# Attention with image prompts on one core: last keys in two column halves, context 1 turned by VectorE, prompt weights and x loaded from the POOL queue, and the last quarter of the first inner products sent ahead

## The chip, the cores and the metric

The kernel runs on one core of a Trainium2 chip. The core has a matrix engine (TensorE, PE in the rows, with PEld for its weight loads), a vector engine (VectorE, DVE), an activation engine (ScalarE, ACT), a general engine (GpSimd, POOL) and a synchronising engine (SyncE, SP) that mostly issues transfers. 16 DMA engines move data between main memory and the core's memories. Each engine works through its own instruction stream in order. The metric is the device time of one execution in microseconds. Three runs of the kernel before took 419.8, 420.98 and 421.6 us; the median is 420.98 us.

## The reference

Eight batches of 112 query rows (320 channels) attend, with 20 heads of 16 channels, to 371 text rows and 4 image-prompt rows of 512 channels. All is float32.

```python
q    = heads(x @ W_q);  k_t = heads(text @ W_k);  v_t = heads(text @ W_v)
p    = softmax(q k_t^T / 4)                       # (b, h, 112, 371)
text_out = p v_t
k_ip, v_ip = heads(ip @ W_k_ip), heads(ip @ W_v_ip)
qsem = l2norm(p text)                             # a 512-vector per (b, h, s)
sem  = qsem . l2norm(ip)                          # (b, h, 112, 4)
p_ip = softmax(q k_ip^T / 4 + 0.5 sem) * spatial_mask
out  = (text_out + p_ip v_ip) @ W_out + b_out + x
```

The kernel never forms qsem. With G = text text^T (the inner products, or Gram matrix), |p text|^2 = p G p^T, and (p text) . ip_n = p (text ip_n), so one product of the probabilities with the columns [G | text ip_n | 1 | V] gives everything that is needed of them.

## The kernel before, in words

**Steps.** A step is (batch b, group g): four heads at a time, five groups to a batch, 40 steps. `scores` (L652) multiplies the masked queries `qm` with the transposed keys `kT`; four heads lie in four 32-row strips of the array, 16 rows of each strip being real and the other 16 masked to zero (two heads share a strip, and r picks one). `probabilities` (L671) takes the maximum on DVE, the exponential on ACT, and SP sends the result p in rows of 32 to the buffer `xg` (`xg<-p`, L686). `transposed` (L688) turns it on DVE in 32x32 blocks into `xgT`. `product` (L703) multiplies `xgT`, block by block, with `u`, which holds [G | text ip_n | 1 | V] for the group. `reduced` (L759) sums product times p on DVE, `value_sums` (L734) copies the rest on ACT. `finish` (L780) makes the output of a batch.

**What feeds u.** `gram` (L463; `first_gram`, L433, for batch 0) computes the inner products, `doubled` scales them into `ug` on ACT and POOL, and `gram_to_groups` (L484) sends each quarter of `ug` with four SP transfers into `u`. `values` (L535) computes V into `vext`; it goes to main memory (`vd`) and comes back by groups (`vr`, `values_to_groups`, L578); `placed` (L625) copies it on POOL into `u`.

**Context.** `ctxT`, the transposed context, is made from `ct`. For batches 0 and 1 `load_ctx` (L135) loads whole rows and `transposed_context` (L394) turns them on PE and copies them out; for batches 2 to 7 the context is loaded in blocks of 32 rows by 128 channels (512-byte pieces, four transfers for the full blocks and four for the last 19 rows) and turned on DVE. `prompts_behind` (L388) lets POOL copy the normalised prompts into the last four columns.

**Keys of the last group.** Channels 256 to 319 hold only four heads. In batches 0 and 7 they come from a product with a widened key weight. In batches 1 to 6 `values` carries 64 extra columns (the key weight's last channels stand beside the value weight in `wv_sb`), POOL spreads them into `k3`, and `keys` (L493) turns them with three PE transposes.

**Order.** PE, SP, DVE, ACT and POOL are written in order by hand, first the prologue (L1020 to L1064), then the steps: `alone` (L1107) for step 0, `pair` (L1115) for two steps at a time, and after every second step `behind` (L1183), which places the coming batch's work: keys `k`, queries `q`, values `v`, inner products `gr`, transposes `tr`, endings `f`. `turn` lists which PSUM pool each next bank is taken from. The prologue's order around the change is

```python
order_values(); drain(products)
gram_to_groups(0, range(QN - 1))          # three quarters
... values(0), queries(0), values_to_dram(0), spread(...), keys(0) ...
values_to_groups(0)
... scores and probabilities of step (0, 0) ...
gram_to_groups(0, (QN - 1,))              # the last quarter
drain(transposed_context(1)); prompts_behind(1)
... scores and probabilities of step (0, 1) ...
load_embed(nc.sync, wkip_sb, w_k_ip); load_embed(nc.sync, wvip_sb, w_v_ip)
transposed(0, 0); placed(0, 0); keys(0); more_constants(); gram(1), first third
```

`project_queries` (L319) begins by letting POOL clear the unused rows of `xT` (L327), which every query product reads.

## Time and profile before

| what | value |
|---|---|
| median of three runs | 420.98 us |
| the profiled execution | 421.54 us |
| its span | 419.8 us |
| PE busy | 411.7 us (98%) |
| PE weight loads busy | 314.1 us (75%) |
| DVE busy | 322.2 us (77%) |
| ACT busy | 185.5 us (44%) |
| POOL busy | 116.0 us (28%) |
| moved by DMA | 64.64 MB in 58002 packets |

A row of the chain or of the timeline gives the start in us, the length in us, the engine, the line and the tile that is written; xN is the number of instructions merged into it, and what stands in brackets is how long the engine stood idle before it and what ended that. A float32 matrix product appears as two PE instructions. PE's ends are modelled from the instruction, so the start of the next piece says more than the end of the last. An SPq or POOLq entry is a queue issuing a transfer.

### The profile page before, as it was taken

To read this page: it belongs to the slowest core of one execution; us is meant where nothing else is said; L and a number is where in the kernel's file an instruction comes from. 1 tells how busy PE (TensorE), PEld (TensorE's weight loads), DVE (VectorE), ACT (ScalarE), POOL (GpSimd) and SP (SyncE) were. 2 spreads that over 40 slices of the span, in tenths; PEclk is the share of its full clock that TensorE was granted. 3 is DMA by queue.
4 is the path that set the end of the run, shared out by engine and by line. 5 is a ranking of instruction groups with operands and counts; after the bars stand their busy time and mean duration, and the time that the engine had idled before them with its cause. 6 is when DMAs were issued, how large, how long until landed. Compare 5 with 4: busy or idle time off the path is not lost.

```text
span 419.8 us, 13826 instructions
## 1 busy us (share of the span) xinstructions
PE 411.7 (98%) x5511; PEld 314.1 (75%) x5511; DVE 322.2 (77%) x684; ACT 185.5 (44%) x634; POOL 116.0 (28%) x278
## 2 busy tenths in 40 slices
PE   8999999999999999999999999999999999999995
PEld 8866686877677786868686877778776888776893
DVE  4054777897887876886888897887788897789964
ACT  3253333334543642514553464333643464246772
POOL 4302310031161352012051225102124126005570
PEclk9999999999999999999999999999999999999999
DMA  8678966778554656577645575575656345575311
GB/s 249 163 190 246 220 157 165 180 187 181 133 156 125 169 127 170 143 162 160 174 116 138 148 173 144 156 186 138 164 150 168 92 118 149 156 177 169 98 34 29
DMA packets 58002, 64.64 MB, mean 154 GB/s; under 512 B 19016, under 2 KB 51760, under 8 KB 57938
## 3 DMA queue, kind: packets, MB, share of 16 engines
q1 hardware_dynamic: 57054, 62.32, 58.5%
q8 instruction: 44, 0.72, 0.7%
q10 hardware_dynamic: 692, 0.89, 0.7%
q0 software_dynamic: 192, 0.55, 0.6%
q14 instruction: 20, 0.16, 0.1%
HBM read 19.04 MB, written 5.22 MB: 58 GB/s over the span
## 4 chain that ended last, share of the span: by engine, by line
PE 87%; DVE 4%; DMA 3%; ACT 2%; SPq 2%; issue 1%; ACTq 0%; POOL 0%; DVEq 0%; POOLq 0%
PE ps_qd L710 39%; PE ps_v L543 15%; PE ps_k L512 10%; PE ps_g L474 8%; PE ps_s L662 5%; PE ps_q L344 3%; PE ps_o L867 2%; DMA xg<-p 1%; DVE xgT L698 1%; PE ps_g L444 1%; DMA vr<-vd 1%; ACT p L679 1%; PE ps_c L414 1%; DVE nmx L675 1%; SPq L488 1%; DMA ct<-in_ctx_dram 1%
## 5 line engine op out<-in xcount | busy, mean ns | idle before, releaser
L710 PE MATMUL ps_qd<-u,xgT 32*112 32x40 f32 (+11 forms) x3840 | 215.7, 351 | 0.4 <-DVE xgT L698 0.4
L710 PEld LDWEIGHTS ps_qd<-u,xgT 32*112 32x112 f32 x3840 | 177.4, 172 | 38.4 <-issue 7.1
L698 DVE STREAM_TRANSPOSE xgT<-xg 128x768 f32<-128x768 f32 (+1 forms) x63 | 123.1, 1976 | 7.1 <-DMA xg<-p 7.1
L679 ACT ACTIVATE p<-ps_s,nmx 112x371 f32<-112x371 f32 x160 | 85.6, 584 | 58.3 <-DVE nmx L675 57.2
L675 DVE TENSOR_REDUCE nmx<-ps_s 112x1 f32<-112x371 f32 x160 | 77.1, 534 | 36.7 <-PE ps_s L662 34.0
L763 DVE CUSTOM_DVE_ANT_0 p<-ps_qd,p 112x371 f32<-112x371 f32 x150 | 72.7, 544 | 15.9 <-ACT pvs L737 10.4
L629 POOL COPY u<-vr 128x64 f32<-128x64 f32 x120 | 26.7, 236 | 185.0 <-PE ps_qd L710 108.0
L543 PE MATMUL ps_v<-wv_sb,ctxT 128*128 128x384 f32 (+1 forms) x192 | 63.8, 479 | 0.3 <-ACT kT L519 0.3
L662 PE MATMUL ps_s<-kT,qm 32*112 32x375 f32 (+1 forms) x320 | 60.8, 486 | 0.0
L543 PEld LDWEIGHTS ps_v<-wv_sb,ctxT 128*128 128x128 f32 x192 | 35.3, 190 | 21.2 <-ACT kT L519 1.2
L512 PE MATMUL ps_k<-ctxT,wk_sb 128*128 128x371 f32 x136 | 45.8, 481 | 0.0
L737 ACT COPY pvs<-ps_qd 112x21 f32<-112x21 f32 x150 | 21.7, 198 | 52.4 <-DVE ss L763 50.1
L512 PEld LDWEIGHTS ps_k<-ctxT,wk_sb 128*128 128x128 f32 x136 | 24.6, 190 | 13.4 <-ACT ctxT L424 0.5
L474 PE MATMUL ps_g<-ctxT 128*32 128x119 f32 (+11 forms) x672 | 33.3, 344 | 0.6 <-POOL ctxT L390 0.6
L474 PEld LDWEIGHTS ps_g<-ctxT 128*32 128x32 f32 x672 | 25.9, 109 | 8.1 <-issue 4.1
L662 PEld LDWEIGHTS ps_s<-kT,qm 32*112 32x112 f32 x320 | 27.1, 171 | 5.0 <-issue 0.5
L550 ACT COPY vext<-ps_v 128x384 f32<-128x384 f32 (+1 forms) x24 | 11.2, 465 | 37.1 <-PE ps_v L543 37.0
L681 ACT COPY ipl<-ps_s 112x4 f32<-112x4 f32 x140 | 24.0, 172 | 0.0
L353 DVE TENSOR_SCALAR qm<-ps_q,emask 128x224 f32<-128x224 f32 (+1 forms) x25 | 9.0, 398 | 18.5 <-PE ps_q L344 18.5
L460 ACT ACTIVATE ug<-ps_g 128x375 f32<-128x375 f32 (+2 forms) x24 | 9.0, 377 | 29.2 <-DMA ct<-in_ctx_dram 8.4
L519 ACT COPY kT<-ps_k 128x371 f32<-128x371 f32 x17 | 8.0, 469 | 30.5 <-PE ps_k L512 30.5
L402 DVE STREAM_TRANSPOSE ctxT<-ct 128x512 f32<-128x512 f32 x18 | 19.3, 1077 | 0.0
(157 smaller groups left out, 311.6 us busy)
## 6 DMA issues: line engine op xcount, KB each, us to landing
xg<-p SPq DMA_DIRECT2D x158, 162.3 KB
u<-ug SPq DMA_DIRECT2D x128, 99.0 KB
ct<-in_ctx_dram SPq DMA_DIRECT2D x24, 176.0 KB
vip<-vipd SPq DMA_DIRECT2D x7, 560.0 KB
vr<-vd SPq DMA_DIRECT2D x20, 120.0 KB
vd<-vext SPq DMA_DIRECT2D x14, 160.0 KB
vd<-vext SPq DMA_DIRECT2D x28, 40.0 KB
ct<-in_ctx_dram SPq DMA_DIRECT2D x4, 256.0 KB
```

Of the source, the lines that this page charges most:

```text
L474: nc.tensor.matmul(ps[p * RG : (p + 1) * RG, s0 : T - t0], ctxT[:, e, t0 + q * RG : t0 + (q + 1) * RG], ctxT[:, e, t0 + s0 : T], start=(e ...
L512: nc.tensor.matmul(ps[:, :TT], wk_sb[:, e, i * P : (i + 1) * P], s["ctxT"][:, e, :TT], start=(e == 0), stop=(e == NE - 1),)
L543: nc.tensor.matmul(ps[:, :w], ctxT[:, e, c * P : (c + 1) * P], wv_sb[:, e, :w], start=(e == 0), stop=(e == NE - 1),)
L629: nc.gpsimd.tensor_copy(region(b, c)[:, :, UV - c * P :], s["vr"][:, c * QN : (c + 1) * QN, g, :])
L662: nc.tensor.matmul(ps[:S, :w], qm[a * RG : (a + 1) * RG, i, r, j * S : (j + 1) * S], s["kT"][a * RG : (a + 1) * RG, i, :w], start=True, st ...
L675: nc.vector.tensor_reduce(nmx, ps[:S, :TT], AX.X, ALU.max, negate=True)
L679: nc.scalar.activation(p, ps[:S, :TT], AF.Exp, bias=nmx)
L681: nc.scalar.copy(s["ipl"][:, groups[g][a], :], ps[:S, TT:T])
L698: nc.vector.transpose(xT[:, j : j + n].rearrange("p j (k q) -> p q j k", q=QN), xg[:, :, j * RG : (j + n) * RG].rearrange("p q (j k) -> p ...
L710: nc.tensor.matmul(banks[a][:S, j * RG : UW], xT[a * RG : (a + 1) * RG, j, :S], region(b, c)[a * RG : (a + 1) * RG, p, q * RG :], start=(j ...
L737: nc.scalar.copy(s["pvs"][:, h, :], ps[:S, TT:UW])
L763: nc.vector.tensor_tensor_reduce(out=p, in0=ps[:S, :TT], in1=p, scale=1.0, scalar=0.0, op0=ALU.mult, op1=ALU.add, accum_out=s["ss"][:, h : ...
```

## The change

Six things change together.

1. The last group's keys. The 64 extra value columns, `k3`, `spread` and the transposes go. For every batch `last_keys` multiplies the 64 key-weight columns with the context's first 186 columns into PSUM partitions 0 to 63 and with the other 185 into 64 to 127, and four ACT copies put both halves twice into `kT`, so that partitions 64 to 127 repeat the four heads. The scores of that group take r = a // 2, and a third masked query product is made.
2. Context 1 is loaded in 32-row blocks and turned on DVE, like batches 2 to 7, and that comes right behind the first inner products, before the transfers to `u`.
3. All four quarters of the first inner products go to `u` at once, ahead of values and probabilities of step (0, 0).
4. The prompt weights and x[1:5] are loaded from the POOL queue, before the last third of the first inner products; x[5:] from the POOL queue in batch 2.
5. All of `gram(1)` is done in the prologue. The prompt projection writes four column tiles of 160 columns in place of two of 320, with three ACT copies and two transfers.
6. ACT is asked for the Sqrt table right behind the key copies, ahead of the Sqrt.

```diff
-    groups.append([2 * HC + a for a in range(GROUP)])
+    groups.append([2 * HC + 2 * (a % 2) + a // 2 for a in range(GROUP)])
...
-    def spread(eng, t):
-
-        v = t[:, :, FULL * P :].rearrange("p k (a r d) -> p k a r d", r=2, d=D)
-        for a in (3, 2, 1):
-            eng.tensor_copy(v[:, :, a, 0, :], v[:, :, a // 2, a % 2, :])
-        eng.memset(v[:, :, :, 1, :], 0.0)
...
-        if b >= LEAD:
+        if b > 0:
...
         ps = bank("ps_kv")
         for e in range(NE):
             for i, w in enumerate((wkip_sb, wvip_sb)):
-                nc.tensor.matmul(
-                    ps[i * N : (i + 1) * N, :C],
-                    ipT[:, e, :],
-                    w[:, e, :],
-                    start=(e == 0),
-                    stop=(e == NE - 1),
-                )
...
+                for n, part in enumerate(parts):
+                    m = 2 * i + n
+                    nc.tensor.matmul(
+                        ps[m * N : (m + 1) * N, : C // 2],
+                        ipT[:, e, :],
+                        w[:, e, part],
+                        start=(e == 0),
+                        stop=(e == NE - 1),
+                    )
...
-        nc.sync.dma_start(vipd, kv[N:])
+        for n, part in enumerate(parts):
+            m = 2 + n
+            nc.sync.dma_start(vipd[:, part], kv[m * N : (m + 1) * N, : C // 2])
...
-            for r in range(2 if i < FULL else 1):
+            for r in range(2):
...
-        if b >= LEAD:
+        if b > 0:
...
             if c == NT - 1:
                 nc.gpsimd.tensor_copy(ctxT[:, :, TT:T], ipnT[:, :, :NIP])
+                load_embed(nc.gpsimd, wkip_sb, w_k_ip)
+                load_embed(nc.gpsimd, wvip_sb, w_v_ip)
+                nc.gpsimd.dma_start(x_sb[:, 1:5, :], x[1:5].rearrange("b s c -> s b c"))
             c0, c1 = c * P, min(c * P + P, T)
...
-        for i in range(NC):
-            ps = bank(f"ps_k_{b}_{i}", spare=0 < b < B - 1 and i == FULL)
-            if 0 < b < B - 1 and i == FULL:
-
-                for c in range(NT):
-                    rows = min(P, TT - c * P)
-                    nc.tensor.transpose(
-                        ps[:, c * P : c * P + rows],
-                        s["k3"][:rows, c].rearrange("p a r d -> p (a r d)"),
-                        ident[:rows, :rows],
-                    )
-                nc.scalar.copy(s["kT"][:, i, :TT], ps[:, :TT])
-                yield
-                return
+        for i in range(FULL):
+            ps = bank(f"ps_k_{b}_{i}")
...
+        last_keys(b, bank(f"ps_k_{b}_{FULL}", spare=0 < b < B - 1))
+        yield
 
     def last_keys(b, ps):
 
         s = st[b]
         for e in range(NE):
-            nc.tensor.matmul(
-                ps[:, :TT],
-                wk_sb[:, e, FULL * P :],
-                s["ctxT"][:, e, :TT],
-                start=(e == 0),
-                stop=(e == NE - 1),
-            )
-        nc.scalar.copy(s["kT"][:, FULL, :TT], ps[:, :TT])
+            for n in range(2):
+                nc.tensor.matmul(
+                    ps[n * REST : (n + 1) * REST, : min((n + 1) * KH, TT) - n * KH],
+                    wk_sb[:, e, FULL * P :],
+                    s["ctxT"][:, e, n * KH : min((n + 1) * KH, TT)],
+                    start=(e == 0),
+                    stop=(e == NE - 1),
+                )
+        for n in range(2):
+            t = slice(n * KH, min((n + 1) * KH, TT))
+            for m in range(2):
+                nc.scalar.copy(
+                    s["kT"][m * REST : (m + 1) * REST, FULL, t],
+                    ps[n * REST : (n + 1) * REST, : t.stop - t.start],
+                )
 
...
-        w = C + REST if 0 < b < B - 1 else C
...
                 nc.tensor.matmul(
-                    ps[:, :w],
+                    ps[:, :C],
                     ctxT[:, e, c * P : (c + 1) * P],
-                    wv_sb[:, e, :w],
+                    wv_sb[:, e, :],
...
-            nc.scalar.copy(vext[:, c, :w], ps[:, :w])
-            if w > C and c == NT - 1:
-                nc.gpsimd.tensor_copy(
-                    s["k3"][:, :, :, 0, :],
-                    vext[:, :, C:].rearrange("p c (a d) -> p c a d", d=D),
-                )
+            nc.scalar.copy(vext[:, c, :], ps[:, :C])
...
+        if i == FULL:
+            r = a // 2
         nc.tensor.matmul(
             ps[:S, :w],
             qm[a * RG : (a + 1) * RG, i, r, j * S : (j + 1) * S],
...
     order_values()
     drain(products)
-    gram_to_groups(0, range(QN - 1))
+    drain(transposed_context(1))
+    gram_to_groups(0, range(QN))
     run(("v", 0), lambda: values(0))
     run(("q", 0), lambda: project_queries(pairs[0]), 3)
     run(("v", 0), None, 2)
     values_to_dram(0, nc.scalar)
-    spread(nc.gpsimd, wq_sb)
-    nc.gpsimd.tensor_copy(wv_sb[:, :, C:], wk_sb[:, :, FULL * P : C])
-    spread(nc.gpsimd, wk_sb)
+    nc.gpsimd.tensor_copy(wq_sb[:, :, C:], wq_sb[:, :, FULL * P : C])
...
-    gram_to_groups(0, (QN - 1,))
     run(("q", 0), None)
-    turn[:] = ["mm", "qd", "qd"]
-    drain(transposed_context(1))
-    prompts_behind(1)
     for a in range(GROUP):
         scores(0, 1, a, early=True)
         probabilities(0, 1, a)
-    load_embed(nc.sync, wkip_sb, w_k_ip)
-    load_embed(nc.sync, wvip_sb, w_v_ip)
     transposed(0, 0)
     placed(0, 0)
     run(("k", 0), None, 2)
     more_constants()
-    run(("g", 1), lambda: gram(1))
+    turn[:] = ["mm", "mm", "sc"]
+    run(("g", 1), lambda: gram(1), NT)
     prologue.close()
...
         if b % 2 == 0 and g == 0:
             if n == 0:
-                turn[:] = ["sc", "mm", "qd", "mm"]
-                nc.sync.dma_start(x_sb[:, 1:5, :], x[1:5].rearrange("b s c -> s b c"))
+                turn[:] = ["qd", "mm"]
             else:
                 turn[:] = ["qd"] * 4 + ["mm"]
                 k(b)
+                nc.scalar.preload_act_table(AF.Sqrt)
                 f(b - 1)
                 if b - 1 < B - 2:
                     prompt_values(b - 1)
             if n:
                 gr(nb)
             tr(0)
-            gr(nb, 2)
             if n:
+                gr(nb, 2)
                 f(b - 1)
             else:
                 run(("pp",), prompt_projections)
@@ -1232,8 +1211,8 @@
                 run(("pp",), None)
             tr(1)
             values_to_dram(nb, nc.sync)
-            if b == 0:
-                nc.sync.dma_start(x_sb[:, 5:, :], x[5:].rearrange("b s c -> s b c"))
+            if b == 2:
+                nc.gpsimd.dma_start(x_sb[:, 5:, :], x[5:].rearrange("b s c -> s b c"))
...
             k(b)
+            nc.scalar.preload_act_table(AF.Sqrt)
             k(nb)
```

More of the change, by code (lines that the diff above doesn't have):

```diff
@@ L52 @@
     HN = H * NIP
+    KH = (TT + 1) // 2
     VW = NIP + 1 + D
@@ L104 @@
     wq_sb = const.tile([P, NC, CP], F32, tag="wq_sb", name="wq_sb")
-    wk_sb = const.tile([P, NE, CP], F32, tag="wk_sb", name="wk_sb")
-    wv_sb = const.tile([P, NE, C + REST], F32, tag="wv_sb", name="wv_sb")
+    wk_sb = const.tile([P, NE, C], F32, tag="wk_sb", name="wk_sb")
+    wv_sb = const.tile([P, NE, C], F32, tag="wv_sb", name="wv_sb")
     wip = work.tile([P, UCOL], F32, tag="u", name="wip")
@@ L241, in order_values @@
             )
-        nc.vector.tensor_copy(
-            wv_by[:, :, :, 2 * FULL, :],
-            wv_in[:, :, FULL * P :].rearrange("p e (a d) -> p e a d", d=D),
-        )
+        last = wv_in[:, :, FULL * P :].rearrange("p e (u v d) -> p e u v d", v=2, d=D)
+        for v in range(2):
+            nc.vector.tensor_copy(wv_by[:, :, 2 * v : 2 * v + 2, 2 * FULL, :], last[:, :, :, v, :])
+    parts = [slice(n * C // 2, (n + 1) * C // 2) for n in range(2)]
     def normalised_prompts():
@@ L279, in prompt_projections @@
             for i, w in enumerate((wkip_sb, wvip_sb)):
-                nc.tensor.matmul(
-                    ps[i * N : (i + 1) * N, :C],
-                    ipT[:, e, :],
-                    w[:, e, :],
-                    start=(e == 0),
-                    stop=(e == NE - 1),
-                )
-        kv = work.tile([2 * N, C], F32, tag="vip", name="kv", bufs=1)
-        nc.scalar.copy(kv, ps[: 2 * N, :C])
-        k3p = k3[:N, 0]
-        nc.gpsimd.tensor_copy(
-            k3p[:, :, 0, :], kv[:N, FULL * P :].rearrange("n (a d) -> n a d", d=D)
-        )
+                for n, part in enumerate(parts):
[7 more added lines that the diff above has]
+                    )
+        kv = work.tile([P, CP], F32, tag="vip", name="kv", bufs=1)
+        nc.scalar.copy(kv[:N, parts[0]], ps[:N, : C // 2])
+        nc.scalar.copy(kv[:N, parts[1]], ps[N : 2 * N, : C // 2])
+        nc.scalar.copy(kv[2 * N :, : C // 2], ps[2 * N :, : C // 2])
+        nc.gpsimd.tensor_copy(kv[:N, C:], kv[:N, FULL * P : C])
         yield
@@ L643, in prompt_logits @@
                 qT[:, i, :],
-                kipb[:, i, heads, :],
+                kipb[:, i, :hn, :],
                 start=True,
@@ L956, in ending @@
             )
-        parts = [slice(i * C // 2, (i + 1) * C // 2) for i in range(2)]
         ps_o = [bank(f"ps_o_{b}_0", spare=True)]
```

15 lines of the change are left out of this document (3 added, 12 removed).

## The prediction

> **What bounds the kernel now.** I read the page first: the busy times, and the chain that ended last by engine.
>
> ```profile
> PE 411.7 (98%) x5511; PEld 314.1 (75%) x5511; DVE 322.2 (77%) x684; ACT 185.5 (44%) x634; POOL 116.0 (28%) x278
> PE 87%; DVE 4%; DMA 3%; ACT 2%; SPq 2%; issue 1%; ACTq 0%; POOL 0%; DVEq 0%; POOLq 0%
> ```
>
> TensorE (PE) is busy 98% of the span and carries 87% of the chain, so a microsecond of matrix work normally counts as one microsecond of time. The exceptions are the stages in which another engine hands PE its input late. The edits touch one such stage: the prologue and the first two steps. So next I read the chain in order of time, prologue first (start, length, what):
>
> ```profile
> 26.07 1.43 PE ps_c L414 x12
> 28.70 5.18 PE ps_k L512 x16
> 33.89 2.64 PE ps_g L474 x27
> 36.53 1.15 PE ps_qd L710 x10
> 41.88 2.19 PE ps_g L474 x43
> 44.07 2.21 PE ps_kv L280 x16
> 46.28 2.78 PE ps_v L543 x8
> 49.05 1.15 PE ps_qd L710 x10
> ```
>
> The prologue is one unbroken string of PE work. The products of step (0,0) begin at 36.53 and those of step (0,1) at 49.05. Then the same view from the steady loop and the last batch, and one row of the timeline:
>
> ```profile
> 101.51 0.32 PE ps_k L503 x3
> 101.83 2.51 PE ps_k L512 x8
> 104.34 5.16 PE ps_v L543 x16
> 138.09 0.47 PE ps_k L503 x3
> 138.56 4.64 PE ps_g L474 x71
> 143.19 2.78 PE ps_v L543 x8
> 359.44 2.17 PE ps_v L543 x8
> 31.43 0.47 ACT L519 COPY kT<-ps_k 128x371 f32<-128x371 f32 x1 [0.57 <-PE ps_k L512]
> ```
>
> **Prices on PE.** A value chunk of 384 columns takes 5.16 / 2 = 2.58 us, one of 320 columns 2.17 us. The 64 columns taken away are worth 0.41 us a chunk, and a column costs 2.17 / (8 x 320) = 0.85 ns in each of a chunk's 8 passes. The three transposes that made the last keys take 0.32 us among full-width work and 0.47 us behind the products, so entering from another tile shape costs about 0.15 us. The chunk at 143.19 (behind the inner products, which use 32-column tiles) takes 2.78 against 2.58, so leaving a column tile costs 0.20 us.
>
> The new last keys issue 4 x 2 matrix products (16 passes) of 186 columns on two 64-column halves of the array. The row of the prompt projection shows what two column tiles side by side cost: 16 passes of 320 columns in 2.21 us, where one after another would take 16 x 320 x 0.85 = 4.35 us. Full overlap it is, so the new last keys cost 8 x 186 x 0.85 = 1.26 us. No row has 64-column tiles; if they did not overlap it would be 2.52 us.
>
> The Trainium skill, TensorEngine Tiling, Key Properties, says that changing the tiling mode drains the engine. The rows agree, at 0.15 to 0.20 us a change.
>
> **The loop, batches 1 to 6.** Values: 18 chunks lose 0.41 us; the first of them lies in a stretch that VectorE (DVE) will set (below), so 17 x 0.41 = 7.0 us are saved. Last keys: in batches 1, 3, 5 they stand between full-width products, so 1.26 + 0.15 + 0.20 replaces 0.32, which is +1.29 each; in 2, 4, 6 they stand between products and inner products, both tiled anyway, so 1.26 + 0.15 replaces 0.47, +0.94 each. Together +6.7 us. Net -0.3 us, near nothing. ScalarE (ACT) now copies the last keys in four pieces; at no more than the 0.47 us of the one whole copy that is at most 4 x 0.47 - 0.47 = 1.4 us more a batch. In batches 1, 3, 5 the scores that read them come only after a key piece and two value chunks (2.5 + 4.3 us of PE), in the others later still, so I take 0; with that cover gone it would be 1.4 us a batch, and a gain is excluded since the work only grows. The Sqrt table asked for earlier, the third mask product on DVE and the last x load, now on POOL, lie on engines at 44, 77 and 28% and off the chain: 0.
>
> **Batch 7.** Its last keys fall from 2.6 to 1.4 us, but DVE sets that stretch of the tail, so 0.
>
> **The prologue.** PE loses the 12 transposes of context 1 (1.43 us) and, in the keys of batch 0, half of one of the two pieces in 5.18 us: 2.59 becomes 1.41, so -1.18. It gains the rest of the inner products of batch 1, brought forward from 41.88 (2.19 us). Products of (0,0) would start at 36.53 - 1.43 - 1.18 + 2.19 = 36.11. They also need their transposed probabilities:
>
> ```profile
> 26.41 3.72 SPq L686 DMA_DIRECT2D xg<-p  x4
> 30.18 2.48 SPq L488 DMA_DIRECT2D u<-ug  x4
> 32.74 3.12 DVE L698 STREAM_TRANSPOSE xgT<-xg 128x768 f32<-128x768 f32 x2 [2.51 <-DMA xg<-p]
> 42.11 0.54 DVE L763 CUSTOM_DVE_ANT_0 p<-ps_qd,p 112x371 f32<-112x371 f32 x1 [2.11 <-ACT pvs L737]
> 43.97 3.00 DVE L698 STREAM_TRANSPOSE xgT<-xg 128x1536 f32<-128x1536 f32 x1
> 14.53 7.77 SPq L488 DMA_DIRECT2D u<-ug  x12
> 24.26 1.88 SPq L582 DMA_DIRECT2D vr<-vd  x4
> 34.51 0.59 POOL L629 COPY u<-vr 128x64 f32<-128x64 f32 x3 [17.05 <-DMA u<-ug]
> ```
>
> The last quarter's four transfers cost SyncE (SP) 2.48 us. Moved ahead, they fill the gap between 14.53 + 7.77 = 22.30 and 24.26, and only some 0.5 us of them pushes the values and probabilities; the first half of the transposes ends near 34.8, before 36.1. So the move itself is hidden, and its gain is too: PE is not waiting for the last quarter at 36.53.
>
> Behind (0,0) PE has only the prompt projection (four tiles of 160 columns, half of 2.21: 1.1 us) and one value chunk (2.17 + 0.20) left, so it is free at 36.11 + 5.35 + 1.1 + 2.4 = 45.0. Step (0,1) needs the transposes of 3.00 us, which stand on DVE behind the reductions of (0,0): 46.97 now, and 0.42 less then, 46.6. PE waits there 1.6 us, and step (0,1) begins 2.4 us earlier than 49.05. That is the whole gain of the start, unless the start itself is held up.
>
> **What holds it up.** POOL works in written order. Context 1 is now turned by DVE from 32x32 blocks, and POOL's copy of the prompts behind it must wait for the last of three such transposes. Behind that copy stands POOL's clearing of xT, which the query product at 20.3 reads:
>
> ```profile
> 14.56 0.28 POOL L327 MEMSET xT<- 64x224 f32 x1
> 17.25 0.20 POOL L390 COPY ctxT<-ipnT 128x16 f32<-128x16 f32 x1
> L402 DVE STREAM_TRANSPOSE ctxT<-ct x18: 1018/1090/1142, 74.5 to 329.3; 128x512 f32<-128x512 f32 x18
> 20.30 0.82 PE L344 MATMUL ps_q<-xT,wq_sb 128*128 128x112 f32 x6
> ```
>
> From the landing of context 1 it takes 3 x 1.09 + 0.20 + 0.28, with some 0.15 of handing over 3.9 us, until that product can run. It is late by L = landing + 3.9 - 20.3, zero up to 16.4 us. When does context 1 land? (Windows: last two columns are the DMA share and GB/s; then the queues' packets, MB and share in 48 to 49 and, two rows, in 50 to 51 us.)
>
> ```profile
> 11.00:12.00 1.00, 1.00 (x12) 1.00 (x11) 0.00 (x0) 0.06 (x1) 0.00 (x0) 1.00 1.06 385
> 12.00:13.00 1.00, 1.00 (x12) 1.00 (x11) 0.00 (x0) 0.59 (x2) 0.45 (x1) 1.00 0.89 242
> 13.00:14.00 1.00, 1.00 (x9) 0.92 (x8) 0.00 (x0) 0.48 (x2) 0.45 (x1) 1.00 0.23 57
> q1 hardware_dynamic: 391, 0.19, 118.5%
> q0 software_dynamic: 27, 0.14, 64.7%
> q1 hardware_dynamic: 195, 0.09, 55.5%
> 47.13 0.92 POOL L118 DMA_DIRECT2D wo_sb<-in_L_xattn_W_out_dram  x1
> 12.51 0.45 POOL L461 TENSOR_TENSOR ug<-ug,half 128x128 f32<-128x128 f32 x1 [3.84 <-ACT ug L460]
> ```
>
> Now its 0.76 MB (371 x 512 floats) are the last thing in a saturated stretch; counted back through 0.06, 0.24 and 0.39 MB in these three windows they began near 10.8 and were there soon after 13. In block form it is 371 rows x 4 pieces = 1484 packets of 512 bytes; context 2, loaded in that form, ran at 391 packets a microsecond, so 3.8 us: 14.6 if alone, L = 0. But it is not alone: where POOL now idles 3.84 us up to 12.51, from 8.67 on, it will issue both prompt weights and x[1:5], 1.88 MB (2 x 512 x 320 and 4 x 112 x 320 floats), which at 0.92 us each fits that gap. The first POOL load now is issued at 47.13 and its queue (q0) is seen carrying data from 50 on, some 2.8 us later, so these join at 11.5, when 3.1 us of context 1 are still to come. At 385 GB/s they need 5 us, at x's shorter rows rather 6, so the landing lies between 14.6 and 20.6, and L between 0 and 4.2. In 50 to 51, when q0 came in beside context 2, q1 fell from 391 to 195 packets, which is half: 3.1 us become 6.2, landing 17.7, L = 1.3. But context 2 was also running out by then, and of the two shares q0 has the larger. I take the middle between 1.3 and the 4.2 that applies if q0 is served first: L = 2.8.
>
> **Sum.** -2.4 (start) -0.3 (loop) +2.8 (late query product) = +0.1 us on the profiled 421.54, 421.6; the median of the three runs, 420.98, stands 0.56 lower, so 421.1. A measurement here can tell about 0.5%, 2.1 us, from no change.
>
> **Rivals.**
> In time: context 1 lands before 17.0 (L under 0.6), because POOL's loads begin later than 11.5 or take turns kindly. For it: at 47.13 q0 took 2.8 us to start, and context 1's own queue is the older. Against it: the DMA share is 1.06 when they meet. The time is 421.0 - 2.7 + 0.3 = 418.6, and 418.3 with L at zero. Faster.
>
> Starved: the small packets of context 1 yield more than a fair share to q0's large ones. In a fifth of a microsecond at 50.6 (the two rows of that window) it was
>
> ```profile
> q0 software_dynamic: 6, 0.03, 73.0%
> q1 hardware_dynamic: 19, 0.01, 30.7%
> ```
>
> 19 packets are 95 a microsecond, a quarter of 391. At that rate the 1210 packets left at 11.5 last to 24.2, L is 7.8, and the time 421.0 - 2.7 + 7.8 = 426.1; it decides against the change once the landing passes 21.2 (L over 4.8). Against it: 5 to 6 us of q0 traffic cannot hold the queue that long, unless both run slower together; part of the fall is context 2 ending. The Trainium skill, DMA: Bandwidth & Descriptors, Queues, rings and completion order, says that an engine takes turns between its queues packet by packet; 27 packets for 0.14 MB against 195 for 0.09 MB agree with large packets against small. By that rule the time would be this rival's.
>
> Halves not side by side: 64-column tiles run one after another. Seven batches (batch 7 is under cover) at +1.26 us give 421.1 + 8.8 = 429.9. Against it: the prompt projection's 2.21 us.
>
> The last quarter does nothing: already in the sum, since the placing that waits 17.05 us for it, at 34.51, does so under cover of PE work.
>
> **How the numbers follow.** Around the sum (L from 0.6 to 4.8, within 0.5%): 0.37. In time: 0.31. Starved: 0.25. Halves in sequence: 0.07. So faster 0.31, same 0.37, slower 0.32. The likeliest case alone spans 418.9 to 423.1. For 8 in 10 the range takes in the first rival, with 0.8 us for loop terms priced at 0, and nearly all of the second short of its own figure: 417.5 to 425.8.
>
> **What would show it.** The query product's start (now 20.3) and what PE waited for: POOL, with DVE and then context 1's transfer behind it. Products of (0,0) at 36.1 + L, of (0,1) at 46.7 + L with PE idle before them and DVE's transposes as the releaser. Last-key rows of 1.3 to 1.5 us in the chain, value chunks at 2.2. Wrong would be: last keys at 2.6, a loop whose period changes by over 0.5 us a batch, or a query product at 20.3 with no gain at 49.

## The result

The changed kernel takes 426.26 us (424.6 to 426.8), the kernel before 420.78 (a fourth run lowers its median from 420.98): a ratio of 1.0132 [1.0105, 1.0159], slower by 1.3%, and 0.5 us above the predicted range. A ratio, here and below, leaves out the few slow executions, among them one of 836 us in the run with the weights between. The profiled execution took 426.62 us with a span of 424.9, so 5.1 us more than the 421.54 and 419.8 of before.

The chain of waits of the changed kernel from 10 to 57 us (start, duration, what):

```profile
10.55 13.30 DMA ct<-in_ctx_dram
...
27.06 0.27 POOL xT L319
...
27.37 0.77 PE ps_q L336 x2
28.14 4.79 PE ps_k L494 x8
...
36.97 2.69 PE ps_k L494 x8
39.66 1.40 PE ps_k L511 x14
41.06 4.64 PE ps_g L468 x70
45.70 1.15 PE ps_qd L696 x10
...
53.23 2.88 DVE xgT L684
...
56.25 1.22 PE ps_qd L696 x10
```

What starts at 27.37 is the last of the query product's three passes over the channels, the one that reads the rows that POOL clears; the other two ran at 20.30, as in the kernel before. It stands behind POOL's clearing of xT, and that behind DVE's three transposes of context 1, which begin only at 23.71. The first keys behind it take 4.79 us where they took 2.62. DVE's transposes, the waits (total, times, longest), the page's row of granted clock and one microsecond behind the wait (its third figure from the end is the granted clock) show it:

```profile
23.71 3.00 DVE L393 STREAM_TRANSPOSE ctxT<-ct 128x512 f32<-128x512 f32 x3 [13.63 <-DMA u<-ug]
POOL ctxT L381 <- DVE ctxT L393: 12.3, 1, 12.3
PE ps_q L336 <- POOL xT L319: 6.5, 1, 6.5
PEclk9979999999999999999999999999999999999999
28.00:29.00 1.00, 1.00 (x3) 0.64 (x3) 0.57 (x2) 0.21 (x1) 0.00 (x0) 0.50 0.66 155
```

PE waits 6.5 us for POOL, POOL had waited 12.3 for DVE. The profile puts DVE's own wait down to a transfer to u, but the trace also counts up to 16 completions for a transfer, and they show another cause: what came in at 23.6 is the last of context 1's four large transfers, those of the full blocks, issued at 8.94. Of its 16 completions 12 were there by 16.8, the others came at 18.7, 20.0, 20.9 and 23.6. The four transfers of the last 19 rows have one completion each, at 21.4, 23.9, 24.3 and 24.7.

The third slice (21 to 32 us) has a clock of 0.7, and in each microsecond from 27 to 32 it is 0.50: PE comes back at half the clock. The Trainium skill, TensorE: Matmul & The Clock Gate, part 1, says that the clock drops to half after an idle window of about 3.4 us; these rows agree, with 0.50 behind a wait of 6.5 us.

Where the 5.1 us are: step (0,1) starts its products 7.20 us later (56.25 for 49.05), the last pair of steps of batch 6 6.06 later, the last products 6.66 later, from these rows of the two chains, after and before:

```profile
367.67 1.15 PE ps_qd L696 x10
409.93 4.94 PE ps_qd L696 x84
421.30 0.60 DVE ob L983 x2
```

```profile
361.61 1.15 PE ps_qd L710 x10
403.27 4.94 PE ps_qd L710 x84
414.64 0.60 DVE ob L998 x2
```

So the loop up to there won 1.14 us, and 0.60 was lost from there to the last products. The rest is the transfer of the last output: from the last addition to the end of the span it is 3.0 us after and 4.56 before. No part of the change touches that transfer; why it was shorter here is not shown.

### The profile page after: what moved, and what is told of

The parts are those of the page before. It is cut to its first block, busy times and chain, and to the rows that moved or that the text cites. A ratio compares the mean times of both kernels' runs of the same rounds, so it can differ in the third digit from the quotient of the medians.

```text
span 424.9 us, 14046 instructions
## 1 busy us (share of the span) xinstructions
PE 410.1 (97%) x5609; PEld 319.9 (75%) x5609; DVE 327.0 (77%) x692; ACT 190.3 (45%) x658; POOL 115.1 (27%) x267
## 4 chain that ended last, share of the span: by engine, by line
PE 82%; DMA 7%; DVE 6%; issue 1%; ACT 1%; SPq 1%; ACTq 0%; POOL 0%; DVEq 0%; POOLq 0%
PE ps_qd L696 39%; PE ps_v L533 11%; PE ps_k L494 10%; PE ps_g L468 8%; PE ps_s L648 6%; PE ps_q L336 3%; DMA ct<-in_ctx_dram 3%; DVE xgT L684 3%; PE ps_k L511 2%; PE ps_o L853 2%; DMA wq_sb<-in_L_xattn_W_q_dram 2%; DVE p L749 1%; DMA xg<-p 1%; DMA vd<-vext 1%; DMA u<-ug 1%
## 5 line engine op out<-in xcount | busy, mean ns | idle before, releaser
L696 PEld LDWEIGHTS ps_qd<-u,xgT 32*112 32x112 f32 x3840 | 179.3, 172 | 37.8 <-issue 6.4
L533 PE MATMUL ps_v<-wv_sb,ctxT 128*128 128x320 f32 x192 | 56.1, 439 | 0.3 <-ACT kT L501 0.3
L494 PEld LDWEIGHTS ps_k<-ctxT,wk_sb 128*128 128x128 f32 x128 | 24.2, 199 | 14.2 <-issue 3.0
L393 DVE STREAM_TRANSPOSE ctxT<-ct 128x512 f32<-128x512 f32 x21 | 22.1, 1063 | 13.6 <-DMA u<-ug 13.6
L540 ACT COPY vext<-ps_v 128x320 f32<-128x320 f32 x24 | 10.2, 427 | 35.8 <-PE ps_v L533 33.3
L667 ACT COPY ipl<-ps_s 112x4 f32<-112x4 f32 x140 | 24.2, 173 | 0.0
L336 PE MATMUL ps_q<-xT,wq_sb 128*128 128x224 f32 (+1 forms) x90 | 17.8, 335 | 6.5 <-POOL xT L319 6.5
L336 PEld LDWEIGHTS ps_q<-xT,wq_sb 128*128 128x128 f32 x90 | 14.8, 194 | 8.8 <-POOL xT L319 6.7
L455 POOL TENSOR_TENSOR ug<-ug,half 128x128 f32<-128x128 f32 (+1 forms) x24 | 10.8, 449 | 35.3 <-ACT ug L454 35.3
```

Of the source, the lines that this page charges most:

```text
L336: nc.tensor.matmul(ps[:, : n * S], wq_sb[:, j, i * P : (i + 1) * P], xT[:, j, : n * S], start=(j == 0), stop=(j == NC - 1),)
L494: nc.tensor.matmul(ps[:, :TT], wk_sb[:, e, i * P : (i + 1) * P], s["ctxT"][:, e, :TT], start=(e == 0), stop=(e == NE - 1),)
L533: nc.tensor.matmul(ps[:, :C], ctxT[:, e, c * P : (c + 1) * P], wv_sb[:, e, :], start=(e == 0), stop=(e == NE - 1),)
L667: nc.scalar.copy(s["ipl"][:, groups[g][a], :], ps[:S, TT:T])
L696: nc.tensor.matmul(banks[a][:S, j * RG : UW], xT[a * RG : (a + 1) * RG, j, :S], region(b, c)[a * RG : (a + 1) * RG, p, q * RG :], start=(j ...
```

## Experiments: the loads, their queue and the clock

Each ratio is against runs of the kernel before on the same chip. The first four kernels share one chip.

**Loads on SP.** The three early loads on SP's queue, at the same place:

```diff
-                load_embed(nc.gpsimd, wkip_sb, w_k_ip)
+                load_embed(nc.sync, wkip_sb, w_k_ip)
...
-                nc.gpsimd.dma_start(x_sb[:, 1:5, :], ...)
+                nc.sync.dma_start(x_sb[:, 1:5, :], ...)
```

> The changed kernel with its three early loads (both prompt weights and x[1:5]) issued by SP at the same place of the program instead of POOL, so that they stand in one queue behind context 1. Three theories. Turns: POOL's queue starves all of context 1's transfer. Tail: it starves only the four pieces of the last 19 rows. Block form: context 1 in 512-byte pieces is this late by itself. Turns and tail: context 1 lands near 16 us, the first query product starts at 20.3 to 21.5 in place of 27.4, and the time falls to 418 to 421 (the transfers to u now queue behind 1.9 MB, which may give back 1 to 2 us). Block form: the product stays at 26 or later and the time within 1 us of 426.

428.27 us, ratio 1.0189 [1.016, 1.0218]. Context 1 is turned from 17.8 on and the query product comes at 21.23 without a wait, so the block form is not late by itself. But the expected gain in time is missed by 7 us, for now u and the rows of xg are late; the chain:

```profile
34.94 2.92 DMA u<-ug
...
39.55 1.26 DMA xg<-p
...
46.34 2.25 PE ps_qd L696 x10
```

**The context's last rows in two pieces.** A row count of 371 leaves 19 rows behind eleven blocks of 32; here they are fetched as 16 and 3:

```diff
+                mid = 16 if b == 1 else TT - full * RG
...
-                    ehs[b, full * RG : TT, a * P : (a + 1) * P],
+                    ehs[b, full * RG : full * RG + mid, a * P : (a + 1) * P],
...
+                if full * RG + mid < TT:
+                    nc.sync.dma_start(v[a * RG + mid : ...], ehs[b, full * RG + mid : TT, ...])
```

> The changed kernel with each 19-row remainder of context 1 loaded in two transfers, of 16 rows and of 3; POOL's loads stay. Tail (19 rows fall to one or few DMA engines, where they wait their turn behind POOL's large packets; 16 rows spread over all): most of context 1 is there before POOL's data begins at 14.4, so the query product starts by 22 and the time is 418.5 to 420.5. Turns: nothing is gained, 425 to 427, product at 26 or later.

424.64 us, 1.0101 [1.007, 1.0132], but the last pass of the query product is at 27.37 as before the edit: context 1 is no earlier. The transfer that ends DVE's wait, 9.90 to 23.15, is the last of the four large ones (the pieces of 16 and 3 rows are issued from 10.41 on), and the last of the added transfers is itself issued only at 23.16. So this run can't tell whether the last rows alone can hold the context up; the run with smaller packets, below, shows that they can.

**Loads later on POOL.** The same three lines behind POOL's prompts copy of batch 1 (issued from 21.8 us):

> The changed kernel with the three loads still on POOL's queue, but issued behind POOL's copy of the prompts of batch 1, so after context 1 has landed. Turns and tail: the query product starts at 20.3 to 21.5, step (0,1) begins near 47, time 418 to 420. Block form: product at 26 or later, time 425 to 427.

426.36 us, 1.0137 [1.0104, 1.017]. The last pass of the query product is at 21.48, as expected, and again the delay only moves on, and the expected gain in time does not come:

```profile
24.61 9.81 DMA u<-ug
...
35.56 3.07 DMA xg<-p
...
44.12 2.25 PE ps_qd L693 x10
```

**The clock by itself.** 30 idle 128x128 products on PE, which are no part of the computation, ahead of the delayed query product:

```diff
+    awake(30)
```

> The changed kernel with 30 idle matrix products of 128 columns on PE in the stretch where it waits for the first query product, so that its clock stays up; they are not part of the computation. If the lower clock after the wait is worth time, the first keys of batch 0 fall from 4.8 to 2.6 us and the time by 2 us, to 424. If another chain (context 1, values and probabilities) sets the start of step (0,0), the time stays within 0.7 us of 426.

423.8 us, 1.0083 [1.0056, 1.011]:

```profile
20.41 6.70 PE ps_w L422 x60
27.11 0.66 PE ps_q L336 x6
27.77 2.51 PE ps_k L494 x8
...
43.04 1.15 PE ps_qd L696 x10
```

The product is as late as in the changed kernel, but the keys take 2.51 instead of 4.79 and step (0,0) starts 2.66 earlier. The lost clock is worth about 2.5 us of the 9.2 by which that step was late.

## Experiments: undoing one part

Four kernels on one chip. **Loads back** is the changed kernel with the loads where the kernel before has them:

```diff
-                load_embed(nc.gpsimd, wkip_sb, w_k_ip)
-                load_embed(nc.gpsimd, wvip_sb, w_v_ip)
-                nc.gpsimd.dma_start(x_sb[:, 1:5, :], ...)
...
         probabilities(0, 1, a)
+    load_embed(nc.sync, wkip_sb, w_k_ip)
+    load_embed(nc.sync, wvip_sb, w_v_ip)
...
                 turn[:] = ["qd", "mm"]
+                nc.sync.dma_start(x_sb[:, 1:5, :], ...)
```

> The two prompt weights are issued on SP behind the probabilities of step (0,1), and x[1:5] on SP behind step (0,0), where the kernel before has them; all else is as in the changed kernel. Theory (1.88 MB too early in a saturated prologue, wherever issued): context 1 is in by about 17.4 us, its DVE transposes run near 17.7, the first query product is at 21 to 22, u's quarters and vr are in by 34, step (0,0) starts its products at 36.5 to 38.5, step (0,1) at 47 to 48.5, and the time is 418.5 to 420.5 us. Rival (the hold-up on POOL and context 1's block form cost by themselves, whatever else is on the queues): the query product stays at 25 or later and the time at 424 or more. Rival (the last quarter ahead of the values is the cost): vr lands after 36 and step (0,0) starts after 40, time 422 to 424.

419.13 us, 0.9966 [0.9946, 0.9986]: 0.3% faster than the kernel before. Its chain:

```profile
20.50 0.47 PE ps_q L336 x2
...
37.00 1.22 PE ps_qd L693 x10
...
44.57 2.88 DVE xgT L681
47.59 1.22 PE ps_qd L693 x10
```

PE waits 0.22 us for POOL ahead of the query's last pass, and the keys behind it start no later than in the kernel before (20.97 for 21.12). Step (0,1) starts 1.46 earlier and waits for DVE.

**Quarter back.** Only the last quarter's move is undone:

```diff
-    gram_to_groups(0, range(QN))
+    gram_to_groups(0, range(QN - 1))
...
         probabilities(0, 0, a)
+    gram_to_groups(0, (QN - 1,))
```

> Only the last quarter of batch 0's inner products goes back behind the probabilities of step (0,0); the loads stay early on POOL. Theory (the early loads cost, the quarter's place does not): the query product stays at 27 to 27.6 us, step (0,1) within 0.7 us of the changed kernel's 56.25, the time 425.5 to 427. Rival (the quarter takes the place of vr and of the rows of xg in the queues): vr and xg land 2 us earlier or more, step (0,1) starts at 54.5 or earlier, time 424.5 or less.

426.4 us, 1.0129 [1.0103, 1.0155]; step (0,1) at 56.15. Beside the early loads the move does nothing that can be told.

**Loads and quarter back.**

> The loads and the last quarter both at their places of before. Theory: within 0.6 us of the run with the loads alone moved back (the quarter costs and brings nothing once the queues have room), 418.5 to 420.5 us. Rival (the quarter's place matters): 1 us or more from that run.

422.33 us, 1.0026 [1.0002, 1.005], 3.2 us above the loads alone: the theory's miss. Step (0,0) starts at 37.01 in both; what is late is a weight of the prompt projection, which with gram(1) in the prologue PE asks for at 43.3 (timeline of PE, in brackets the idle time before):

```profile
45.54 2.35 PE L273 MATMUL ps_kv<-wip,ipT 128*32 128x160 f32 x28 [1.80 <-DMA wip<-in_L_xattn_W_v_ip_dram]
47.82 4.34 PE L530 MATMUL ps_v<-wv_sb,ctxT 128*128 128x320 f32 x8
52.09 1.22 PE L693 MATMUL ps_qd<-u,xgT 32*112 32x392 f32 x10
```

The weights are issued at 37.44 here and at 36.37 with the quarter ahead; the second is in at 45.5 here and at 42.8 there, and the clock falls again (values 4.34 for 2.42). So the last quarter's move is worth something here because it clears the queue ahead of the weights.

**Context 1's turning back.** DVE's transposes and POOL's prompts copy behind step (0,0)'s probabilities, so that nothing on POOL holds the query product:

```diff
-    drain(transposed_context(1))
     gram_to_groups(0, range(QN))
...
     run(("q", 0), None)
+    drain(transposed_context(1))
```

> Only the DVE transposes of context 1 and POOL's prompts copy go back behind the probabilities of step (0,0); the loads stay early on POOL. Theory (the loads starve whatever is on the queues at the time): the query product comes at 20.5 to 21.5 us without a wait on POOL, yet u, vr and the rows of xg land late (xg past 38), step (0,0) starts at 41 to 44, step (0,1) at 53 to 56, the time is 423.5 to 426. Rival (POOL's hold-up was the only cost): step (0,1) at 48 or 49, time 419 to 420.5.

426.37 us, 1.0133 [1.0097, 1.0168], as slow as the changed kernel. The chain shows the second way in which the late context costs:

```profile
7.32 16.61 DMA ct<-in_ctx_dram
23.95 0.51 SPq L482
...
34.69 2.94 DMA vr<-vd
...
43.14 2.25 PE ps_qd L696 x10
```

SP's next transfer to u is issued only at 23.95, when the third of context 1's large transfers (issued at 7.32) is in, and vr and xg stand behind it. In the trace eight completion counters go round among these transfers, and each issue first waits until the transfer that had its counter last is in. So the stop stands in SP's instructions; that the queue itself would stop is not shown.

## Experiments: which pair it is

**Early loads in the kernel before.** Of the whole change only the loads, in the kernel before:

> The kernel before, and of the change only the three early loads: prompt weights and x[1:5] on POOL behind the prompts copy of batch 0, in place of SP behind step (0,1)'s probabilities and behind step (0,0). Context 1 in its old form and the last quarter in its old place. Theory (1.88 MB too early starves whatever the queues carry between 14 and 25 us): u, vr and the rows of xg land 4 us later or more, step (0,0) starts its products at 40 to 43 (before: 36.5), step (0,1) at 52 to 55 (before: 49.0), time 423.5 to 427 us. Rival (the loads cost only together with the block form of context 1 and POOL's hold-up): step (0,1) at 50 or earlier, time below 422.

420.55 us, 0.9984 [0.9953, 1.0014]: no cost that can be told. The theory so far, that 1.88 MB too early starves whatever is on the queues, falls: step (0,0) starts at 35.99. What differs above all is the context's form: this kernel fetches context 1 in whole rows. In the microsecond from 12 the two queues together moved 0.37 MB here (rows: packets, MB, share of 16 engines), and 0.17 MB in the changed kernel, at a share no lower:

```profile
q1 hardware_dynamic: 149, 0.26, 78.8%
q0 software_dynamic: 21, 0.11, 35.7%
```

```profile
q1 hardware_dynamic: 344, 0.17, 122.1%
```

**By dose.** The run with the loads back, but with the weights issued between the two steps' probabilities, or with only x[1:5], or only the weights, early on POOL:

> As the run with the loads moved back, but the two prompt weights on SP between the probabilities of step (0,0) and those of step (0,1). With gram(1) in the prologue the prompt projection comes at 43.2 us, some 6 us behind the issue of the weights there. Theory (room in the queues from 33 us on, and the rows of step (0,1) are needed only at 44.5): step (0,0) at 36.5 to 37.5, step (0,1) at 47.2 to 48, time 418 to 419.8. Rival (the 1.31 MB delay the rows of step (0,1) past 44.5 or hold back the probabilities): step (0,1) at 48.5 or later, time 420 to 422.

> As the run with the loads moved back, but x[1:5] (560 KB) early on POOL as in the changed kernel. Theory (cost goes with the bytes put ahead): 0.3 of the changed kernel's 1.88 MB, so the query product comes at 21 to 23.5 us, time 419.5 to 422. Rival (any early load on POOL holds the context up by its larger packets, whatever their number): query product at 25 or later, time 423 or more.

> As the run with the loads moved back, but the two prompt weights (1.31 MB) early on POOL as in the changed kernel. Theory (cost goes with the bytes put ahead): 0.7 of the changed kernel's 1.88 MB, so the query product comes at 23 to 26 us, time 422.5 to 425. Rival (x[1:5], whose packets are smaller and more, is what starves the context): query product at 22 or earlier, time below 421.

Weights between: step (0,1) at 47.85, ratio 1.0017 [0.9984, 1.0049] (median 421.83), so the trace is as the theory has it, and the time isn't told from that of the kernel before. x alone: query product at 22.64, step (0,1) at 49.33, 419.81 us, 0.9972 [0.9935, 1.0009]. Weights alone: 25.50 and 54.28, 424.6 us, 1.0052 [1.0011, 1.0093]; three of its ten executions took 420.6, the others 424.4 to 426.4, so the loss does not come every time. In the profiled executions, one for each, it goes with the bytes, in the order 0, 0.57, 1.31 and 1.88 MB: the last pass of the query product is at 20.5, 22.6, 25.5, 27.4.

**Rows in the changed kernel, pieces in the kernel before.** The first has context 1 in whole rows, turned by PE, with all else of the change; the second is the kernel before with the early loads and context 1 in 512-byte pieces, turned where PE turned it:

```diff
# rows in the changed kernel
-        if b > 0:
+        if b > 1:
...
-    drain(transposed_context(1))
...
+    turn[:] = ["mm", "qd", "qd"]
+    drain(transposed_context(1))
+    prompts_behind(1)
# pieces in the kernel before (with the early loads)
-        if b >= LEAD:
+        if b > 0:
```

> The changed kernel with context 1 fetched in whole rows and transposed by PE behind step (0,0)'s probabilities, as in the kernel before; early loads on POOL and the last quarter ahead stay. New theory (it is the pair that costs: context 1 in 512-byte pieces moves 140 to 190 GB/s at full queues between 12 and 14 us, where whole rows moved 335 with the same loads early, so that its end falls behind the loads and holds POOL, and SP's next issues): query product at 20 to 21.5 us, step (0,0) at 36.5 to 38.5, step (0,1) at 47.3 to 49.5, time 418.5 to 421. Rival (the old one: the loads and sixteen transfers to u ahead of vr are too much for the queues in any form of context 1): step (0,0) at 40 or later, time 423 or more.

> The kernel before with the early loads and, beside them, context 1 in 512-byte pieces, transposed by DVE behind step (0,0)'s probabilities (so nothing of it stands ahead of the first query product on POOL or DVE). New theory (the pair): context 1 lands at 22 to 24 us, SP's transfers to u wait for it, vr and the rows of xg come 3 us late or more, step (0,0) at 39.5 to 44, time 423 to 427. Rival (the late context costs by POOL's hold-up of the query product alone): step (0,0) at 37.5 or earlier, time 421.5 or less.

Rows in the changed kernel: 421.42 us, 1.0012 [0.9987, 1.0037], 5 us less than the change. Pieces in the kernel before: 424.4 us, 1.0072 [1.0042, 1.0102], 4 us more than the same loads with rows. Its chain:

```profile
9.08 13.86 DMA ct<-in_ctx_dram
22.96 0.51 SPq L491
...
39.18 0.25 POOL u L632
39.47 1.64 PE ps_qd L713 x10
```

The rows' time lies 0.4 us above its expected range: step (0,0) starts at 39.99, since the rows of xg, behind sixteen transfers to u and vr, land at 38.1. So early loads and the quarter ahead do crowd the queue a little in any form.

**Smaller packets.** Each early load cut in two halves of columns, to make POOL's packets as small as the context's:

> The changed kernel with each of the three early loads on POOL cut in two halves of columns, so that its packets have 640 bytes instead of 5120 and 1280; the bytes are the same. Theory (the engines share their time packet by packet, so the context's 512-byte pieces got 0.09 of the bytes beside the weights' packets): context 1 gets nearly half the bytes, its DVE transposes start at 17.5 to 20 us, the query product comes at 21.5 to 23.5, time 419.5 to 423.5. Rival (what holds the context up is the number of bytes queued ahead of its last pieces, or SP's late issue of them, not the size of the other packets): transposes at 22 or later, time 424.5 or more.

425.81 us, 1.0121 [1.0097, 1.0145], third transpose at 24.27. The edit did little of what it was for: in 16 to 17 us POOL's queue moved 0.35 MB in 103 packets, 3.4 KB each on average, and 0.36 MB in 77, 4.7 KB, in the changed kernel. But the run shows what the last rows do. The large transfers are in early, and DVE's first two transposes run at 16.72 and 17.75; the third waits for the last transfer of 19 rows alone, issued at 13.02:

```profile
13.02 11.17 DMA ct<-in_ctx_dram
24.27 1.09 DVE ctxT L393
```

It also shows how the two queues share. The first two rows are 17 to 18 us of this run, when only the last rows of context 1 are left: 6 packets of SP's queue stand beside 97 of POOL's, one in sixteen. The other two are 16 to 17 us of the run with pieces in the kernel before, when a large transfer is still on all its engines (its 16 completions come from 20.4 to 22.95): 68 stand beside 64.

```profile
q0 software_dynamic: 97, 0.33, 92.6%
q1 hardware_dynamic: 6, 0.00, 0.9%
q0 software_dynamic: 64, 0.30, 83.6%
q1 hardware_dynamic: 68, 0.03, 12.5%
```

Both counts fit engines that take turns between the queues packet by packet: all 16 of them in the second case, one in the first, which agrees with the single completion of each 19-row transfer. By bytes the pieces get a tenth (0.03 beside 0.30 MB).

**The fourth combination, and the winner again.** Rows with the loads back, and loads back once more, on one chip:

> The changed kernel with context 1 in whole rows and with the three loads at their places of before: the fourth of the four combinations of form and loads. Theory (only the pair is dear: pieces beside early loads): rows without the loads cost PE's 12 transposes, 1.4 us, and win nothing over pieces without the loads; query product at 20 to 21.5 us, step (0,0) at 37 to 38.5, time 419 to 421. Rival (the rows are the better form on any queue): step (0,0) at 36.5 or earlier and the time below that of the pieces without the loads on the same chip by 0.5 or more.

> The run with the loads moved back once more, word for word, on another chip and beside the rows. Theory: faster than the kernel before by 0.2 to 0.6 per cent, query product at 20.3 to 21, step (0,1) at 47.3 to 48.2, time 418.3 to 420. Rival (its 0.34 per cent hung on one chip, as the weights land at 42 to 44.5 us and PE asks for them at 43.2): ratio 0.999 or more.

420.08 us, 0.9978 [0.995, 1.0005], and 419.63 us, 0.9975 [0.9947, 1.0002]. The four ratios of the changed kernel:

| context 1 | loads early on POOL | loads as before |
|---|---|---|
| 512-byte pieces | 1.0132 | 0.9966, 0.9975 |
| whole rows | 1.0012 | 0.9978 |

Pieces cost 1.2% beside the early loads and nothing that can be told without them. PE's 12 transposes (1.43 us) don't show in the time either: in rows and in pieces step (0,1) starts at 47.39, where DVE sets it. The second chip's interval for the winner just reaches no change; taken together, some 0.3% is likely and half a per cent is not.

**Half of DVE's transposes ahead.** With the loads back, the first half of step (0,1)'s transposes ahead of step (0,0)'s reductions:

```diff
+        if n == 0:
+            transposed(*steps[1], 0, BLK // 2)
```

> The run with the loads moved back, and the DVE transposes of step (0,1) in two halves, the first ahead of step (0,0)'s reductions, where DVE stood idle from 40.5 to 42.6 us. Theory (the start of step (0,1) at 47.6 is set by DVE: reductions to 44.5, then 2.88 of transposes; PE ends the values at 46.9): step (0,1) at 46.9 to 47.1, time 0.4 to 0.7 below that run, 418.2 to 419.2. Rival (its rows land after 41, so the first half holds the reductions up): step (0,1) at 47.5 or later, time 419 to 420.5.

422.01 us, 1.0025 [1.0007, 1.0043]: no gain, and slower than the loads back alone. DVE did it in its idle time (40.76 to 42.3), but PE then waited for the prompt weights, and step (0,1) began at 47.86. A second loss shows later, rows of xg that land at 91.57, behind which DVE and ACT come late and PE stands idle 1.8 us up to 94.76; why those rows were late there was not found out.

```profile
44.30 1.28 PE L273 MATMUL ps_kv<-wip,ipT 128*32 128x160 f32 x28 [0.31 <-DMA wip<-in_L_xattn_W_v_ip_dram]
```

## Why the prediction was wrong

The prediction said 421.1, range 417.5 to 425.8, with no change as its likeliest case. The step that failed is the term "late query product", L = 2.8, taken as "the middle between 1.3 and the 4.2 that applies if q0 is served first". By the prediction's own measure L was 7.07 (27.37 - 20.30). Four things under it were off:

- The upper bound. "At 385 GB/s they need 5 us ... so the landing lies between 14.6 and 20.6". POOL's 1.88 MB were seen from 14.0 to 24.1, which is 186 GB/s, and the large transfer that DVE waited for was in at 23.6. The queues together ran near the bound's rate for three microseconds only (375, 354 and 357 GB/s from 16 to 19), and it left out what the small pieces get meanwhile: about one for each POOL packet of ten times their size, and that on few engines once most of them are through.
- The start. The loads were to join at 11.5, 2.8 us behind their issue as at 47.13; their data is seen from 14.0, 5.5 us behind the issue at 8.59. It did not help: 423 packets a microsecond of SP's queue became 23 (rows of 13 to 14, and 16 to 17 us), and the pieces left at 15 us took 9 us more.
- Even alone the pieces land later than the 14.6 worked out: with the loads back DVE starts on them at 16.76, and PE waits 0.22.
- Only the last of the query's three passes reads the cleared rows, so PE's wait is 6.48 and not 7.07.

```profile
q1 hardware_dynamic: 423, 0.21, 122.5%
q0 software_dynamic: 77, 0.36, 94.9%
q1 hardware_dynamic: 23, 0.01, 3.9%
```

The second miss is a term that was not there: what a wait of that length does to PE's clock, 2.47 us (keys 4.79 - 2.62, query 0.77 - 0.47).

The rest of the sum held, in one place by luck. Step (0,0) was put at 36.11 + L: with 7.07 and 2.47 that is 45.65, measured 45.70. But the wait is 0.59 shorter than this L, and the work of PE ahead of step (0,0), which was to shrink by 0.42 (36.53 to 36.11), did not shrink: from the end of the first keys to these products it takes 12.77 (32.93 to 45.70) where it took 12.79 (23.74 to 36.53), as the scores of step (0,1) take 1.70 in place of 1.21, a term put at nothing. The two errors nearly cancel. Step (0,1) was to follow 10.5 later, set by DVE's transposes: 10.55. Last keys 1.41: 1.40. Value chunks 2.17: 2.15 to 2.40. The loop's -0.3 came out as -1.14, of which 0.66 is no term of the sum: in the kernel before a wait for vr near 180 us makes the stretch from step (2,3) to (3,0) 21.74 us (166.48 to 188.22), two batches on it is 21.08. The other 0.48 is near the 0.3. The end, priced at 0, took 0.60 more. From 421.6: +4.27 (L), +2.47 (clock), -0.84 (loop, beyond the -0.3), +0.60 (end), -1.56 (last output) is 426.5, against the profiled 426.62.

Of the rivals, "Starved" had mechanism and size (L of 7.8, 426.1), at a chance of 0.25; "5 to 6 us of q0 traffic cannot hold the queue that long" was the wrong argument against it, as that traffic took 10. Its own reason, that large packets take turns with small, fits the counts: 68 beside 64 with pieces of a large transfer left, 6 beside 97 with the last rows alone, and in the changed kernel 23 beside 77, in between. The Trainium skill, DMA: Bandwidth & Descriptors, Why a DMA increments its semaphore by 16 and not by 1, says that a transfer runs on as many engines as the largest number up to 16 that divides its outer sizes; for the last 19 rows that is one. The trace agrees: each of these transfers has a single completion, and in the run with smaller packets they alone hold context 1 up to 24.2. In the changed kernel a large transfer was as late (23.6); why 4 of its 16 completions lagged so far behind the other 12 stays open. The time of "In time" comes once the loads are away: 418.6 predicted, 419.13 and 419.63 measured. "Halves not side by side" is refuted by the 1.40.

"Hidden, and its gain is too" held for the last quarter beside the early loads (1.0129 without the move, 1.0132 with it). Without them it missed 3.2 us: the prediction did not ask what stands behind the quarter on SP, the prompt weights, for which PE now asks 6 us after their issue.

## What to carry to other kernels

Where a queue is full, price an early load by what is still on the queue when its data comes, not by its own bytes: the same 1.88 MB cost a few tenths of a per cent at most beside a context in whole rows (371 of 2 KB) and some 1 to 1.6% beside one in 512-byte pieces (1484 of them). Count what is left in packets, each of which may wait for one large packet of the other queue, and look for a transfer whose rows fall to a single engine. When two bounds lie far apart, look for what makes the upper one too low, and add to every wait of several microseconds on PE the slow clock behind it, here 2.5 us behind a wait of 6.5. And a move that hides its own cost still shifts what stands behind it on the queue: follow the queue to the next transfer that PE waits for.

## What the hardware showed unasked

- Transfers in 512-byte pieces ran at 0.17 to 0.21 MB a microsecond with the engines full (share 122%); in the same microsecond the kernel with whole rows moved 0.37 MB.
- A load issued by POOL at 8.59 us was first seen moving data at 14.0 on a full queue, 5.5 us later; at 47.13 in the kernel before it was 2.8.
- Beside POOL's packets the 512-byte pieces moved about one for one (68 beside 64 in a microsecond), so with a tenth of the bytes; the last 19 rows, on a single completion, one in sixteen (6 beside 97).
- Late in the prologue one slow transfer stopped SP's issue of others: in two kernels a transfer to u was issued at 22.96 and 23.95, within 0.1 us of the landing of a transfer of context 1 (22.94 and 23.93). Both issues wait in SP's instructions for the counter that this transfer had used.
